# A graph layer with 400,000 edges on one core: gates computed from PSUM, last sums and maps in another order, tile bases kept in PSUM

## The chip, the cores and the metric

The kernel runs on one core of one Trainium2 chip. The metric is device time in microseconds (us) of one launch; the number given for a kernel is the median of its runs. The engines are PE (TensorE, matrix multiplies), DVE (VectorE), ACT (ScalarE), POOL (GpSimd) and SP (SyncE, which here only starts DMAs). PEld is the weight load of PE.

## The reference

12,500 nodes have 64 scalars and 32 vectors of three components (160 numbers). 400,000 edges, sorted by destination, each have a source, a destination, four numbers (e0 and the vector e1) and 64 numbers that go through a small network to 224 weights w1 to w5. Cut to what matters:

```python
h_s = s @ lin1_ws * a * _inv(64);  h_v = einsum('nci,cd->ndi', v, lin1_wv) * a * _inv(32)
w = silu(edge_scalars @ fc_w1 * _inv(64)) @ fc_w2 * _inv(64)     # split into w1..w5
es, ev = h_s[edge_src], h_v[edge_src]                            # the gather
mid_s = [w1*es*e0,  w4*(ev.e1)*_inv(3)]
mid_v = [(w2*es) x e1,  w3*ev*e0,  w5*cross(ev, e1)*_inv(2)]
agg = segment_sum(mid, edge_dst) / 4                             # the scatter
pre = sc(node) * a + lin2(agg) * a
out = [silu(pre_s[:64]),  sigmoid(pre_s[64:96]) * pre_v]         # 64 + 96 numbers
return layernorm(x + out)
```

## The kernel before

**Stages.** The first stage reads the nodes in seven chunks, multiplies them by lin1 on PE, scales the result on DVE and writes a table `h_tab` of [12500, 160] to DRAM. Between the chunks, `bases` takes the first destination of each group of three edge tiles ("block", 1042 of them), and a matmul with a row of ones spreads them over the partitions; ACT copies the result to the SBUF tile `lo` (L307, L308). When all destinations `dt` are loaded, `rel = dt - lo` (L402, L407) gives every edge its place in a window of 16 nodes.

**The loop.** Edges go in 3125 tiles of 128, in 782 steps of four tiles (the last step has one). The instruction order on PE, DVE, ACT, POOL and SP is written out by hand (`manual_schedule`). A step n does:

- `gather`: four indirect DMAs on POOL (L456), one row of `h_tab` per edge, into one of four buffers `hg`. In 11 of the 782 steps, SP fetches the rows with single DMAs instead (L485).
- `weights`: four matmuls into the PSUM tile `pw` (L498), from `hid`, which `hidden` made two steps earlier (L447 on PE, Silu on ACT, L449).
- `one_hot` (L561), `products` (L508 once, L516 three times) and `select_quad` (L570) on DVE: the 13 pieces of the messages in `pr`, and a selector `sel` with the edge's four numbers.
- `sum_up`: eight matmuls (L577) that add the tiles to `pa`, two steps behind their weights: in step n PE runs `weights(n)` and then the sums of step n - 2.
- When a pair of blocks is complete, ACT copies it (`sa`, L790); PE turns it (L586) two steps later, ACT copies that to `tt` (L589, L591).
- When sixteen blocks are turned, `output` maps the group by lin2 (22 matmuls, L601, copy `os` L604), and DVE adds each block to the window of `acc` that the block's base names (L609). The last groups are cut after the blocks at which 28, 18, 8, 2 and 0 blocks are left.

**Finishing nodes.** `finish` makes a job of four node tiles (24 jobs in the loop, the last of them with two tiles, and one behind it). `turn(k)` transposes one tile of `acc` into the PSUM tile `pp` (L636); one tile is turned per step. The step's DVE list then has, between L508 and the first L516, the scaling of `pp` by the node attribute into `z` in SBUF (L637). The following steps each take one item of the rest: `gates` (Sigmoid on ACT for all four tiles, L643), `gated` (L648, L649), `residual` (L657), `moments` (L662, L664), `root` (Sqrt, L668), `norm` (L672, L674) and the store. `finish` loads the residual rows `xt` when the job begins.

**PSUM.** Eight banks: two `pw` tiles of two banks each, two `pa`, and two `misc` banks taken in turn by `ph`, `pt`, `po`, `pp` and others. PE can write a `misc` bank only when the use before the last has been read.

**Edges of the order.** Behind the loop, the remaining sums, the turns and maps of the last groups, and the last finish job follow in program order.

## Time and profile before

| | |
|---|---|
| median of 3 runs | 3973.56 us (3970.84 to 3974.85) |
| profiled execution | 3976.66 us, span 3974.7 us |
| mean granted clock of PE | 0.968 |
| busy: PE, PEld, DVE, ACT, POOL | 92%, 40%, 61%, 24%, 74% |
| first and last gather start (L456) | 60.46 and 3937.20 us |
| last add to `acc` behind the loop; y of the last job complete | 3953.85; 3958.81 us |
| table loads on ACT | 48 for Silu, 25 for Sigmoid, 25 for Sqrt, 1 other; 1.283 us each |

How to read it: a line of the timeline gives start, duration, engine, line of the kernel, operation, output<-inputs and, in brackets, the idle time before it and what ended it ("issue": nothing that the profile shows). A line of the waits gives the total in us, the number of times and the longest wait. A line of the groups gives busy time, mean ns of one, and the idle time before them.

### The profile page before, as it was taken

What the parts mean: (1) busy time and instruction counts of PE and PEld (TensorE: products, weight loads), DVE (VectorE), ACT (ScalarE), POOL (GpSimd) and SP (SyncE); (2) the same over time, 40 slices, a digit from 0 to 9 for tenths busy, and PEclk for the clock granted to TensorE, in tenths of its full rate; (3) what the DMA queues carried; (4) which work ended last, traced back from release to release, by engine and by line L of the source; (5) the groups of instructions that cost most, each with busy time, mean ns of one, the idle gap of its engine ahead of it and who ended that gap; (6) DMA issues with size and microseconds to landing.
All of it is one profiled execution on the core that took longest, in us unless ns stands there. A gap on an engine that the chain in (4) does not pass through costs nothing. (4 is left out here: it accounts for less than half of the span.)

```text
span 3974.7 us, 58310 instructions
## 1 busy us (share of the span) xinstructions
PE 3659.0 (92%) x14291; PEld 1589.7 (40%) x14291; DVE 2416.5 (61%) x6607; ACT 940.7 (24%) x2463; POOL 2952.7 (74%) x3100
## 2 busy tenths in 40 slices
PE   6899998998999999899989999999999999999897
PEld 4344343343344344334334344343343443344343
DVE  5656665655665665656656556656665665665665
ACT  2222221221222222212212222222221221222222
POOL 4777777777777777777777777777777777777774
PEclk8999999999999999999999999999999999999998
DMA  8343444444444344443443444444444444444432
GB/s 231 96 106 86 111 100 105 98 103 104 99 99 110 95 102 105 100 108 89 107 112 91 105 99 99 107 99 97 110 99 106 99 103 104 99 99 108 99 95 67
DMA packets 243271, 412.51 MB, mean 104 GB/s; under 512 B 83147, under 2 KB 173575, under 8 KB 242023
## 3 DMA queue, kind: packets, MB, share of 16 engines
q0 software_dynamic: 150160, 262.93, 27.0%
q1 hardware_dynamic: 92246, 145.66, 15.6%
q8 instruction: 115, 1.88, 0.2%
q14 instruction: 236, 1.93, 0.2%
q10 hardware_dynamic: 514, 0.10, 0.0%
HBM read 392.43 MB, written 16.00 MB: 103 GB/s over the span
## 5 line engine op out<-in xcount | busy, mean ns | idle before, releaser
L456 POOL DMA_INDIRECT hg<-h_tab,idx x3081 | 2938.5, 954 | 945.3 <-issue 852.6
L498 PE MATMUL pw<-w,hid 128*128 128x448 f32 x3126 | 1367.3, 561 | 157.0 <-DVE sel L570 111.8
L577 PE MATMUL pa<-pr,sel 128*64 128x416 f32 x6250 | 1296.2, 536 | 0.0
L516 DVE TENSOR_TENSOR pr<-pw,hg 128x384 f32<-128x384 f32 x2313 | 1136.1, 546 | 0.0
L508 DVE TENSOR_TENSOR pr<-pw,hg 128x512 f32<-128x512 f32 x771 | 532.6, 691 | 914.4 <-DMA hg<-h_tab,idx 656.8
L498 PEld LDWEIGHTS pw<-w,hid 128*128 128x128 f32 x3126 | 554.7, 194 | 639.1 <-issue 465.6
L577 PEld LDWEIGHTS pa<-pr,sel 128*64 128x64 f32 x6250 | 386.9, 139 | 807.5 <-issue 797.8
L790 ACT COPY sa<-pa 128x416 f32<-128x416 f32 x521 | 263.7, 506 | 1360.4 <-PE pa L577 1357.9
L561 DVE TENSOR_TENSOR pw<-rel,iota 128x64 f32<-128x64 int16 x782 | 179.7, 230 | 535.8 <-PE pw L498 533.5
L447 PE MATMUL misc<-es,w 128*128 128x512 f32 (+1 forms) x784 | 447.2, 653 | 24.0 <-DMA es<-in_es_t_dram 20.8
L449 ACT ACTIVATE hid<-misc 128x512 f32<-128x512 f32 x392 | 233.6, 596 | 722.4 <-PE misc L447 717.8
L586 PEld LDWEIGHTS misc<-ident,sa 128*128 128x128 f32 x2084 | 239.6, 141 | 332.5 <-issue 252.5
L601 PE MATMUL misc<-tt,l 128*96 128x256 f32 (+5 forms) x1496 | 353.0, 384 | 15.2 <-DVE z L637 13.7
L586 PE MATMUL misc<-ident,sa 128*128 128x128 f32 x2084 | 329.1, 281 | 21.0 <-DVE z L637 14.1
L570 DVE TENSOR_TENSOR sel<-pw,eas 128x256 f32<-128x256 f32 x782 | 321.8, 412 | 0.0
L601 PEld LDWEIGHTS misc<-tt,l 128*96 128x96 f32 (+1 forms) x1496 | 231.5, 165 | 155.1 <-issue 76.5
L589 ACT COPY tt<-misc 128x192 f32<-128x192 f32 x521 | 164.8, 316 | 537.4 <-PE misc L586 524.3
L447 PEld LDWEIGHTS misc<-es,w 128*128 128x128 f32 x784 | 118.7, 191 | 286.7 <-issue 227.1
L609 DVE TENSOR_TENSOR acc<-acc,os 96x32 f32 x1042 | 195.4, 187 | 24.3 <-ACT os L604 6.0
L591 ACT COPY tt<-misc 128x64 f32<-128x64 f32 x521 | 116.5, 224 | 0.0
L604 ACT COPY os<-misc 96x512 f32<-96x512 f32 (+2 forms) x68 | 38.3, 564 | 321.6 <-PE misc L601 309.7
L636 PE MATMUL misc<-ident,acc 96*128 96x96 f32 x196 | 36.3, 272 | 55.7 <-DVE pw L561 33.3
(87 smaller groups left out, 680.6 us busy)
## 6 DMA issues: line engine op xcount, KB each, us to landing
es<-in_es_t_dram SPq DMA_DIRECT2D x258, 384.0 KB
hq<-h_tab SPq DMA_DIRECT2D x5632, 0.6 KB
hg<-h_tab,idx POOLq DMA_INDIRECT x3081
h_tab<-ht POOLq DMA_DIRECT2D x6, 1280.0 KB
xt<-in_x_dram SPq DMA_DIRECT2D x23, 320.0 KB
out_dram<-y SPq DMA_DIRECT2D x23, 320.0 KB
xv<-in_xv_t_dram SPq DMA_DIRECT2D x25, 187.5 KB
xs<-in_xs_t_dram SPq DMA_DIRECT2D x25, 125.0 KB
```

The lines of the kernel that those rows point to most:

```text
L447: nc.tensor.matmul(ph[:k, c], w1[:k, :k], es[:k, t0 * P + c0 * P:t0 * P + c1 * P], start=True, stop=True)
L449: nc.scalar.activation(hid[:k, c], ph[:k, c], AF.Silu, scale=1.0 / math.sqrt(64))
L456: nc.gpsimd.indirect_dma_start(out=hg[:, t, :], out_offset=None, in_=h_tab, in_offset=bass.IndirectOffsetOnAxis(ap=i, axis=0))
L498: nc.tensor.matmul(pw[:, t:t + m, :NWT], hid[:m * S, c * P:(c + 1) * P], w2[:m * S, :m], start=True, stop=True)
L508: nc.vector.tensor_mul(two, pw[:, :n, :2 * S].rearrange("p t (k c) -> p t k c", k=2), hg[:, :n, None, :S].to_broadcast([P, n, 2, S]))
L516: nc.vector.tensor_mul(pr[:, :n, first:first + V3].rearrange("p t (i c) -> p t i c", i=3), pw[:, :n, None, 2 * S + k * V:2 * S + (k + 1) * ...
L570: nc.vector.tensor_mul(sel[:, :n], oh[:, :, None, :].to_broadcast([P, n, 4, W]), by_slot(tiles[0][0])[:, u:u + n, :, None].to_broadcast([P ...
L577: nc.tensor.matmul(pa[half * ROWS:(half + 1) * ROWS, :NPR], sel[:, t].rearrange("p k w -> p (k w)"), pr, start=start, stop=stop)
L586: nc.tensor.transpose(pt[:, four * P:four * P + k], sa[:k, c:c + P], ident[:k, :k])
L601: nc.tensor.matmul(po[:, k, :nb], l2[r, terms[to, part, four]], a[:, :nb], start=(n == 0), stop=(n == len(of) - 1))
L609: nc.vector.tensor_add(window, window, os[:, :, b])
L790: nc.scalar.copy(sa, pas.pop(j)[:, :NPR])
```

## The change

It does five things.

- `lo` is a PSUM tile. The matmuls that spread the bases run behind the node stage, the copies on ACT are gone, and L402 and L407 read PSUM.
- `turn(k)` puts Tanh of half the scaled sums straight from `pp` into `g` (SBUF), one call per tile, and returns `gate`: three fused operations on DVE, the first two writing to free columns of the same PSUM bank. sigmoid(z) = (1 + tanh(z/2)) / 2, so (g + 1) * pp, times half the node attribute, plus `xt`, is the residual sum. `z`, `gates`, `gated` and `residual` are gone. A job has its turns and three more items.
- From step 778 on, sums run one step behind their weights.
- In step 780 (n + 2 == 782) no maps and no turns are issued; they follow in step 781, behind the last weights.
- The groups of blocks with 2 and 0 left become one.

```diff
-    lo = ends_pool.tile([P, NB], F32, name="lo")
+    base_f = ends_pool.tile([1, NB], F32, name="base_f")
...
-            for b0 in range(0, NB, U * P):
-                b1 = min(NB, b0 + U * P)
-                ps = nps.tile([P, U, P], F32, name="hp").rearrange("p u c -> p (u c)")
-                nc.tensor.matmul(ps[:, :b1 - b0], ones, base_f[:, b0:b1], start=True, stop=True)
-                nc.scalar.copy(lo[:, b0:b1], ps[:, :b1 - b0])
...
+    lo_ps = ends.enter_context(tc.tile_pool(name="lo_ps", bufs=1, space=PSUM))
+    lo = lo_ps.tile([P, -(-NB // 512) * 512], F32, name="lo")
+    for b0 in range(0, NB, 512):
+        b1 = min(NB, b0 + 512)
+        nc.tensor.matmul(lo[:, b0:b1], ones, base_f[:, b0:b1], start=True, stop=True)
     load_chunk(0, nc.gpsimd)
     nc.gpsimd.dma_start(dt, dst)
+    half_at = consts.tile([P, NT], F32, name="half_at")
+    nc.vector.tensor_scalar_mul(half_at, at, 0.5)
...
-            pp = psum.tile([P, 2, V3], F32, name="pp", tag="misc")
+            pp = psum.tile([P, 512], F32, name="pp", tag="misc")
             for m in range(2):
-                nc.tensor.transpose(pp[:, m], acc[:, m, c:c + P], ident[:V3, :V3])
-            return lambda: nc.vector.tensor_scalar(
-                z[:, k], pp.rearrange("p m c -> p (m c)"), at[:, t0 + k:t0 + k + 1], None,
-                op0=OP.mult)
...
+                nc.tensor.transpose(pp[:, m * V3:(m + 1) * V3], acc[:, m, c:c + P], ident[:V3, :V3])
+            half = half_at[:, t0 + k:t0 + k + 1]
+            nc.scalar.activation(g[:, k], pp[:, :V3], AF.Tanh, scale=half)
+            pg = pp[:, 2 * V3:2 * V3 + D]
+
+            def gate():
+                nc.vector.scalar_tensor_tensor(pg[:, :S], g[:, k, :S], 1.0, pp[:, :S],
+                                               op0=OP.add, op1=OP.mult)
+                nc.vector.scalar_tensor_tensor(
+                    pg[:, S:].rearrange("p (c i) -> p i c", i=3),
+                    g[:, k, None, S:].to_broadcast([P, 3, V]), 1.0,
+                    pp[:, V3:2 * V3].rearrange("p (i c) -> p i c", i=3),
+                    op0=OP.add, op1=OP.mult)
+                nc.vector.scalar_tensor_tensor(y[:, k], pg, half, xt[:, k],
+                                               op0=OP.mult, op1=OP.add)
...
-            if len(turns) == NO or NB - 2 * j - 2 in (28, 18, 8, 2, 0):
+            if len(turns) == NO or NB - 2 * j - 2 in (28, 18, 8, 0):
...
-                if len(waits) > 2:
+                while len(waits) > (2 if n + 4 < len(steps) else 1):
                     sum_up(n, *waits.pop(0))
                 hide(n + 2)
-                for blocks, in due(maps_due, n):
-                    output(n, blocks)
-                for j, sa in due(turns_due, n):
-                    turn_blocks(n, j, sa)
+                if n + 2 != len(steps):
+                    for blocks, in due(maps_due, n):
+                        output(n, blocks)
+                    for j, sa in due(turns_due, n):
+                        turn_blocks(n, j, sa)
```

More of the change, by code (lines that the diff above doesn't have):

```diff
@@ L301, in bases @@
             nc.vector.tensor_copy(rows[:, even:], dt[0:1, even * BT:(NB - 1) * BT + 1:BT])
-            base_f = ends_pool.tile([1, NB], F32, name="base_f")
             nc.vector.tensor_copy(base_f, rows)
-            for b0 in range(0, NB, U * P):
-                b1 = min(NB, b0 + U * P)
-                ps = nps.tile([P, U, P], F32, name="hp").rearrange("p u c -> p (u c)")
-                nc.tensor.matmul(ps[:, :b1 - b0], ones, base_f[:, b0:b1], start=True, stop=True)
-                nc.scalar.copy(lo[:, b0:b1], ps[:, :b1 - b0])
             nc.vector.tensor_sub(share, rows, share)
@@ L615, in finish @@
         whole = nt if p == P else nt - 1
-        spans = [(0, nt)] if t0 + nt == tiles_of_nodes else [(k, k + 1) for k in range(nt)]
         xt = fin.tile([P, most, D], F32, name="xt", bufs=2)
@@ L629, in turn @@
                 held.extend(fin.tile([P, most, *shape], F32, name=name) for name, shape in (
-                    ("z", [2 * V3]), ("sg", [V3]), ("y", [D]), ("st", [6]), ("mv", [2]),
-                    ("rs", [])))
-            z = held[0]
+                    ("g", [V3]), ("y", [D]), ("st", [6]), ("mv", [2]), ("rs", [])))
+            g, y = held[:2]
             c = (t0 + k) * P
-            pp = psum.tile([P, 2, V3], F32, name="pp", tag="misc")
+            pp = psum.tile([P, 512], F32, name="pp", tag="misc")
@@ L635, in turn @@
             for m in range(2):
-                nc.tensor.transpose(pp[:, m], acc[:, m, c:c + P], ident[:V3, :V3])
-            return lambda: nc.vector.tensor_scalar(
-                z[:, k], pp.rearrange("p m c -> p (m c)"), at[:, t0 + k:t0 + k + 1], None,
-                op0=OP.mult)
-        def gates():
-            z, sg = held[:2]
-            nc.scalar.activation(sg[:, :nt], z[:, :nt, :V3], AF.Sigmoid)
-        def gated():
-            z, sg, y = held[:3]
-            for k, m in spans:
-                nc.vector.tensor_mul(y[:, k:m, :S], z[:, k:m, :S], sg[:, k:m, :S])
-                nc.vector.tensor_mul(
-                    y[:, k:m, S:].rearrange("p t (c i) -> p t i c", i=3),
-                    z[:, k:m, V3:].rearrange("p t (i c) -> p t i c", i=3),
-                    sg[:, k:m, None, S:].to_broadcast([P, m - k, 3, V]))
@@ L654, in residual @@
-        def residual():
-            y = held[2]
-            for k, m in spans:
-                nc.vector.tensor_add(y[:, k:m], y[:, k:m], xt[:, k:m])
+                nc.tensor.transpose(pp[:, m * V3:(m + 1) * V3], acc[:, m, c:c + P], ident[:V3, :V3])
[12 more added lines that the diff above has]
+                                               op0=OP.mult, op1=OP.add)
@@ L659, in moments @@
+            return gate
         def moments():
-            _, _, y, st, mv, _ = held
+            _, y, st, mv, _ = held
             for k in range(nt):
@@ L666, in root @@
         def root():
-            mv, rs = held[4:]
+            mv, rs = held[3:]
             nc.scalar.activation(rs[:, :nt], mv[:, :nt, 1], AF.Sqrt, bias=eps)
         def norm():
-            _, _, y, _, mv, rs = held
+            _, y, _, mv, rs = held
             nc.vector.reciprocal(rs[:, :nt], rs[:, :nt])
@@ L679, in finish @@
         return [lambda k=k: turn(k) for k in range(nt)] + [
-            gates, gated, residual, moments, root, norm]
+            moments, root, norm]
     tiles_of_nodes = -(-N // P)
```

## The prediction

> **What bounds the kernel now.** I read the page first, then the waits of each engine, then single stretches of the timeline.

> ```profile
> PE 3659.0 (92%) x14291; PEld 1589.7 (40%) x14291; DVE 2416.5 (61%) x6607; ACT 940.7 (24%) x2463; POOL 2952.7 (74%) x3100
> ...
> L456 POOL DMA_INDIRECT hg<-h_tab,idx x3081 | 2938.5, 954 | 945.3 <-issue 852.6
> ```

> PE is busy 92%, so it looks like the bound. But look at POOL: 3081 gathers of 954 ns, with 945 us idle "before" them that nobody caused. The waits of POOL between 1000 and 2000 us say what that idle time is:

> ```profile
> POOL hg L456 <- issue: 220.2, 722, 0.3
> POOL hg L456 <- DMA hg<-h_tab,idx: 4.9, 16, 0.3
> POOL hg L456 <- DVE acc L609: 4.6, 15, 0.3
> ```

> The third number is the longest wait: 0.3 us everywhere. Every gather starts 0.30 us after the one before it ended; POOL never waits for a free buffer. The first starts at 60.46, the last at 3937.20: 3080 steps of 1.2587 us, where the usual step is 0.947 (median) + 0.305 = 1.252. So the stream of gathers carries 3877 of the 3974.7 us. The time is three terms: when the first gather starts, how long each takes, and the tail behind the last.

> PE comes second. Its waits from 400 to 3890 us (first lines):

> ```profile
> PE pw L498 <- DVE sel L570: 100.1, 65, 5.1
> PE pw L498 <- DVE acc L609: 32.3, 19, 5.2
> ...
> PE misc L601 <- DVE z L637: 13.7, 5, 4.4
> PE misc L586 <- DVE z L637: 13.7, 5, 4.6
> ```

> The list of 400 to 3890 sums to 230 us over 90 finished node tiles, 2.55 us of PE slack per tile. PE keeps up, with little to spare.

> What makes a gather long? The timeline of POOL and DVE at one finishing job:

> ```profile
> 1956.30 0.95 POOL L456 DMA_INDIRECT hg<-h_tab,idx  x1 [0.30 <-issue]
> ...
> 1957.38 0.21 DVE L648 TENSOR_TENSOR y<-z,sg 128x64 f32<-128x64 f32 x1
> 1957.52 0.29 DVE L649 TENSOR_TENSOR y<-z,sg 128x96 f32<-128x96 f32 x1
> 1957.56 2.08 POOL L456 DMA_INDIRECT hg<-h_tab,idx  x1 [0.30 <-issue]
> ...
> 1958.87 0.69 DVE L508 TENSOR_TENSOR pr<-pw,hg 128x512 f32<-128x512 f32 x1
> 1959.48 1.48 DVE L516 TENSOR_TENSOR pr<-pw,hg 128x384 f32<-128x384 f32 x3
> 1959.94 0.95 POOL L456 DMA_INDIRECT hg<-h_tab,idx  x1 [0.30 <-issue]
> ```

> The gather that falls into the eight back-to-back products of `gated` takes 2.08 instead of 0.95. Those products read two SBUF operands. The longer run L508, three L516, L570, with one operand in PSUM, leaves gathers at 0.95. At the start it is the same:

> ```profile
> 67.98 6.38 DVE L402 TENSOR_TENSOR rel<-dt,lo 128x260 int16<-128x260 int32 x12 [14.47 <-DMA dt<-in_dst_dram]
> ...
> 72.81 2.35 POOL L456 DMA_INDIRECT hg<-h_tab,idx  x1 [0.30 <-issue]
> ```

> I went through all 3081 gathers: 74 take over 0.965 us. Above the median, 39 of them lie on L648, L649 or L657 and lose 16.2 us; the four beside L402 (1.29, 1.25, 1.26, 2.35) lose 2.4; the rest, scattered, 1.6.

> **Gates from PSUM.** Removed per tile: L637 (407 ns), L648 (214), L649 (281), L657 (315) = 1.217 us of DVE, the last three with two SBUF operands. Added: one Tanh on 128x96 and three fused operations. No row shows the fused operation: at the price of the plain products it is 214 + 281 + 315 = 0.81 us; at twice the cost per element (1.04 ns by L516, 546 ns for 384) it is 0.81 + 320 x 1.04 ns = 1.14. I take 0.81, since its sizes are those of the rows. DVE saves 0.08 to 0.41 us per tile, worth nothing itself: it is 61% busy. What counts is the operands: the new three read pp, pp and pg in PSUM, with one SBUF tensor each (g, g, xt). By L508, L516 and L570 such operations don't slow a gather, so the 16.2 us go. Bounds: 0 (the slowing is not about operands) to -16.2.

> [...]

> **The longer hold.** pp's bank is one of two in the `misc` rotation. Before, it came free after L637; now after Tanh and three operations: +0.40 (0.81 - 0.41) to +0.73 us per tile. Tanh itself (0.3 us; L643 takes 362 ns for twice the columns) runs while DVE does L561 and L508 (0.9 us). Behind the gate on DVE are the three L516 of that step, and PE's next transposes or maps wait for the bank. Per tile 0.73 stays under PE's 2.55 us. Locally I compared each step's gathers with the end of the products that free their buffer: the margin is 10.6 us in the median, but 0.73 at 2432.5, 1.66 at 82.97, 2.25 at 2437.5 and 2.65 at 1178. Four turns in a row cost up to 2.9 us, so those late places lose 0 to 3 us: I take +1. The gate also needs xt five steps earlier than L657 did. Two of the 25 loads go out only at the first turn (1145.3, 3526.3); in both the next L508 stood idle 6.50 and 5.72 us for its gather, which covers it.

> Table loads: 25 sigmoids in batches become 98 separate Tanh. If Tanh needs its own table beside Silu, that is up to two loads of 1.283 us per tile, 196 loads in place of 50, ACT +187 us, on an engine 24% busy. The Silu reload at 379.64 ended 0.6 us before its operand came, so such loads hide; I take 0.

> [...]

> **Bases in PSUM.** L402 loses one SBUF operand. The four gathers get 2.4 us back, but the 17th gather (82.97) needs the buffer that step 0's products free at 79.92 + 1.47 = 81.39. So 1.5 us count. Its cost: the three banks of `lo` lie under the later pw banks, so the first L498 waits for rel (74.7) instead of running at 68.53. It took 3.35 us there, giving 78.1, and DVE is in the l2 scaling until 79.06: covered. If hid's bank is blocked too, add L447 (2.05) and Silu (0.6 + 0.2): 80.9, step 0 ends 83.2, and the 17th gather slips 0.3. Bounds -2.4 to +0.5; I take -1.5. The broadcast of the bases leaves the node stage, where PE stood from 26 to 33 us; but DMA is at 1.01 to 1.04 of its engines from 10 to 60 us, so the first gather moves by -1.4 (the wait of the last chunk, 51.22) to +1. I take 0. The three copies L308 (1.35 us of ACT) and half_at (one DVE operation in a 14 us wait) cost nothing.

> **Tail.** Counted from 3941.09, when DVE ends step 780. Before, PE had used its wait for that to run ten blocks' maps (3937.23 to 3940.79); then 18 sums, maps (2.44), transposes, maps again (2.31), last add at 3953.85. After, the sums of 779 and the last weights come earlier, but the ten blocks' maps stand behind the sums of 780: 1.62 + 3.56 + transposes 1.2 + last sums 0.4 gives 3947.9. Then copy 0.51, transposes 0.6, copies 0.54, one set of maps 2.44, copy 0.35, eight adds 1.65, gaps 0.3: 3954.3, 0.45 later. The last job took 4.96 us from there to y (3958.81). Now: transposes 0.6, Tanh 0.3, four gates of 0.81 with banks in turn, about 4.35. So -0.6 + 0.45, about -0.2. The queue is long and I modelled it by hand: -2 to +2.

> **Sum.** -16.2 - 1.5 + 1.0 - 0.2 = -16.9 us. The profiled run took 3976.66 (span 3974.7 and 2.0 around it), 3.1 above the median 3973.56; so 3959.8 there, and 3956.7 as a median.

> **Rivals.**
> A, the gathers stay slow: the cause is bursts of short DVE operations, or any use of the second SBUF operand. For it: L561 and L609 also have two SBUF operands, 180 + 195 us busy; if the 20.2 us were spread by busy time, the 82 us that go (94 x 0.81 + 6.4) would return only 3.6. Against it: the long gathers sit on L648 to L657 and L402. Time 3970 to 3974, say 3971.
> B, slower: the bank hold. If Tanh and the Silu behind it each bring an unhidden load (2.57 us) on top of 0.40 to 0.73, PE loses 3.0 to 3.3 per tile. It decides from 2.55 us on: then PE sets the pace, and 94 x (0.45 to 0.75) = 42 to 70 us are added. A cold restart makes it worse: after a 3.06 us wait for z the 22 maps at 2417.86 took 9.81 us, not 5.25. Time about 4030. Against it: loads ran ahead of their operands.
> C, the mechanism holds but the start takes no part and the thin places lose 3: 3961. This lies inside the main case.

> **How the numbers follow.** Main case (with C) 0.80, from 3951.5 (-16.2 - 2.4 - 1.4 - 2) to 3965 (-16.2 + 0.5 + 3 + 1 + 2, rounded up for gathers that stay long). A 0.11, B 0.09. The range reaches a little into A: 3951.5 to 3968. Within 0.2% means 3965.6 to 3981.5, about what a measurement of this kernel can tell from no change: that is A. Faster 0.80, same 0.11, slower 0.09.

> **What would show it.** Right: L456 near 2919 us busy for 3081 gathers, none over 1.3 us in the loop; about 3860 us from first to last gather; POOL's longest wait still 0.3; L561 of step 0 still near 79; the last add some 16 us behind the last gather, as now (16.7 from 3937.20). Wrong: gathers of 1.5 to 2 us beside the new gates (A); POOL waiting microseconds for products, PE waits for the gate growing past 200 us, table loads near 200 (B).

## The result, and the profile after

The changed kernel takes 3962.65 us (median of 11 runs, 3961.70 to 3964.88), against 3973.45 us (11 runs, 3970.57 to 3977.09) for the kernel before in the same comparison. The ratio is 0.9974, 95% interval 0.9965 to 0.9984: 10.8 us less, where 16.9 were forecast. The time lies in the range (3951.5 to 3968). Its profiled execution took 3963.18 us, span 3961.2.

The groups of the page, PE's total and POOL's gathers:

```profile
PE 3650.1 (92%) x14269; PEld 1583.0 (40%) x14269; DVE 2411.7 (61%) x6519; ACT 898.7 (23%) x2484; POOL 2932.3 (74%) x3100
...
L457 POOL DMA_INDIRECT hg<-h_tab,idx x3081 | 2918.0, 947 | 947.7 <-issue 844.0
```

The mean of a gather fell from 954 to 947 ns, that is from 2938.5 to 2918.0 us in all. Of 3081 gathers, 54 take more than 0.965 us, and together they lose 3.4 us; before, 74 lost 20.1. None takes more than 1.10. The timeline at one of the new gates shows why:

```profile
1937.16 0.34 ACT L637 ACTIVATE g<-misc,half_at 128x96 f32<-128x96 f32 x1 [1.09 <-PE misc L635]
1937.22 0.95 POOL L457 DMA_INDIRECT hg<-h_tab,idx  x1 [0.30 <-issue]
1937.87 0.22 DVE L641 SCALAR_TENSOR_TENSOR misc<-g,misc 128x64 f32<-128x64 f32 x1
1938.12 0.26 DVE L643 SCALAR_TENSOR_TENSOR misc<-g,misc 128x96 f32<-128x96 f32 x1
1938.42 0.38 DVE L648 SCALAR_TENSOR_TENSOR y<-misc,half_at,xt 128x160 f32<-128x160 f32 x1
1938.48 0.95 POOL L457 DMA_INDIRECT hg<-h_tab,idx  x1 [0.30 <-issue]
```

Both gathers lie on the gate's operations and keep their 0.95 us.

The waits of POOL from 64 to 3950 us (total, times, longest):

```profile
POOL hg L457 <- issue: 837.3, 2747, 0.3
POOL hg L457 <- DMA hg<-h_tab,idx: 28.0, 92, 0.3
POOL hg L457 <- DVE pr L517: 20.4, 59, 2.8
```

The last line is new: one gather waited 2.8 us for a buffer. It is the 17th; the timeline of the start, with its cause:

```profile
74.05 0.43 DVE L408 TENSOR_TENSOR rel<-dt,lo 128x1 int16<-128x1 int32 x5
74.58 2.04 PE L448 MATMUL misc<-es,w 128*128 128x512 f32 x2 [18.88 <-DVE rel L408]
77.31 3.35 PE L499 MATMUL pw<-w,hid 128*128 128x448 f32 x4 [0.69 <-ACT hid L450]
80.70 0.23 DVE L562 TENSOR_TENSOR pw<-rel,iota 128x64 f32<-128x64 int16 x1 [1.86 <-PE pw L499]
81.57 1.48 DVE L517 TENSOR_TENSOR pr<-pw,hg 128x384 f32<-128x384 f32 x3
83.32 0.94 POOL L457 DMA_INDIRECT hg<-h_tab,idx  x1 [2.75 <-DVE pr L517]
```

Not only the first weights but already the first `hid` (L448) waits until `rel` is done, so step 0's products end at 83.05, and the 17th gather starts behind them.

The waits of PE, 400 to 3880 us:

```profile
PE pw L499 <- DVE sel L571: 56.0, 38, 4.0
PE misc L635 <- DVE pw L562: 54.6, 23, 6.2
...
PE misc L587 <- DVE y L648: 12.9, 8, 4.6
PE misc L602 <- DVE y L648: 11.1, 8, 4.6
```

With 7.6 us of L635, the waits for the gate come to 31.6 us; those for `z` were 37.9. Table loads are 25 for Silu, 25 for Sqrt and 1 other: 98 Tanh added none.

Last, the tail. In the timeline:

```profile
3919.58 0.64 PE L499 MATMUL pw<-w,hid 64*128 64x224 f32 x2
3923.19 3.04 PE L578 MATMUL pa<-pr,sel 128*64 128x416 f32 x8 [2.97 <-DVE pw L562]
3926.16 3.59 PE L602 MATMUL misc<-tt,l 128*96 128x160 f32 x22
...
3937.89 1.74 DVE L610 TENSOR_TENSOR acc<-acc,os 96x32 f32 x8 [4.56 <-ACT os L605]
```

and the windows of that wait and of the sums behind it (busy PE, PEld, DVE, ACT, POOL, then granted clock, DMA share, GB/s):

```profile
3920.22:3923.19 2.97, 0.00 (x1) 0.04 (x1) 2.53 (x7) 0.00 (x0) 0.00 (x0) 0.94 0.50 136
3923.19:3926.20 3.01, 3.01 (x9) 0.86 (x9) 1.08 (x6) 0.00 (x0) 0.00 (x0) 0.50 0.12 23
```

PE waited 2.97 us with nothing to do, the clock was halved behind the wait, and the eight sums of step 780 took 3.04 us instead of 1.62. From the last gather (3919.11) to the last add's end (3939.63) it is 20.5 us; before, 16.65.

### The profile page after: what moved, and what is told of

It is laid out like the page before. It is cut to its first block, busy times and chain, and to the rows that moved or that the text cites. A ratio compares the mean times of both kernels' runs of the same rounds, so it can differ in the third digit from the quotient of the medians.

```text
span 3961.2 us, 58261 instructions
## 1 busy us (share of the span) xinstructions
PE 3650.1 (92%) x14269; PEld 1583.0 (40%) x14269; DVE 2411.7 (61%) x6519; ACT 898.7 (23%) x2484; POOL 2932.3 (74%) x3100
## 5 line engine op out<-in xcount | busy, mean ns | idle before, releaser
L457 POOL DMA_INDIRECT hg<-h_tab,idx x3081 | 2918.0, 947 | 947.7 <-issue 844.0
L499 PE MATMUL pw<-w,hid 128*128 128x448 f32 x3126 | 1360.3, 559 | 116.7 <-DVE sel L571 66.6
L517 DVE TENSOR_TENSOR pr<-pw,hg 128x384 f32<-128x384 f32 x2313 | 1137.4, 547 | 0.0
L499 PEld LDWEIGHTS pw<-w,hid 128*128 128x128 f32 x3126 | 553.8, 194 | 593.9 <-issue 469.3
L562 DVE TENSOR_TENSOR pw<-rel,iota 128x64 f32<-128x64 int16 x782 | 179.4, 229 | 538.7 <-PE pw L499 536.9
L448 PE MATMUL misc<-es,w 128*128 128x512 f32 (+1 forms) x784 | 451.4, 658 | 24.1 <-DVE rel L408 18.9
L448 PEld LDWEIGHTS misc<-es,w 128*128 128x128 f32 x784 | 119.7, 192 | 287.8 <-issue 231.6
L610 DVE TENSOR_TENSOR acc<-acc,os 96x32 f32 x1042 | 194.3, 187 | 29.4 <-ACT os L605 11.1
L635 PE MATMUL misc<-ident,acc 96*128 96x96 f32 x196 | 36.4, 271 | 87.1 <-DVE pw L562 62.0
```

The costliest lines, as they stand in the source:

```text
L448: nc.tensor.matmul(ph[:k, c], w1[:k, :k], es[:k, t0 * P + c0 * P:t0 * P + c1 * P], start=True, stop=True)
L457: nc.gpsimd.indirect_dma_start(out=hg[:, t, :], out_offset=None, in_=h_tab, in_offset=bass.IndirectOffsetOnAxis(ap=i, axis=0))
L499: nc.tensor.matmul(pw[:, t:t + m, :NWT], hid[:m * S, c * P:(c + 1) * P], w2[:m * S, :m], start=True, stop=True)
L517: nc.vector.tensor_mul(pr[:, :n, first:first + V3].rearrange("p t (i c) -> p t i c", i=3), pw[:, :n, None, 2 * S + k * V:2 * S + (k + 1) * ...
L610: nc.vector.tensor_add(window, window, os[:, :, b])
```

## Theories for the experiments

T1: gathers are long where DVE runs back to back through operations with two SBUF operands; the gates from PSUM end that. T2: the rest of the change gives some of it back, by PE's wait in the tail, in which the clock falls. Rivals: gathers are slowed by any use of two SBUF operands, or by any burst (A); the longer hold of the banks costs (B). Some of the runs below were made on chips on which the kernel before takes 5254 to 5338 us, so each is compared only with runs of the kernel before on the same chip. Line numbers of the experiments' kernels differ by a few from those of the changed kernel.

## Experiment 1: the gates alone

The kernel before with the new `turn`, `gate` and `half_at` only:

```diff
+            nc.scalar.activation(g[:, k], pp[:, :V3], AF.Tanh, scale=half)
...
+                nc.vector.scalar_tensor_tensor(y[:, k], pg, half, xt[:, k],
+                                               op0=OP.mult, op1=OP.add)
```

> The gates alone, for a chip on which the kernel before takes about 3,972 us. If the gathers' loss is what the gates free: no gather over 1.1 us beside the gate operations, about 3 us lost in all instead of 20, last gather near 3,919 to 3,921, 16.6 us from the last gather to the last add as before, time 3,956 to 3,960. If the gathers are slow whatever DVE reads: 3,971. On a chip of the other sort: from no difference to 0.4% slower, as before.

Measured: 3958.10 us (6 runs, 3956.44 to 3958.93) against 3970.66 (10 runs); ratio 0.9968, interval 0.9956 to 0.998. The page's group of gathers:

```profile
L458 POOL DMA_INDIRECT hg<-h_tab,idx x3081 | 2916.5, 947 | 944.7 <-issue 839.5
```

50 gathers over 0.965 us lose 3.3 us, none is above 1.10 beside a gate. Three at 1.25 to 1.26 are left at the start, where the operation on `rel` still reads two SBUF tensors; the whole change has none there. The last gather starts at 3915.88, 3 us earlier than forecast, with no wait of POOL above 0.3 us. So the gates alone bring 22.0 us of gather time, 16.8 of it from gathers over 0.965 us, and the whole gain. That the old gates made gathers long and the new ones don't is shown by an edit that touches nothing else; A's time, 3971, is refuted. Which property of the old gates did it is not shown by this run. The edit moves an operand to PSUM, but it also breaks up the run of eight products, and the new operations no longer overlap: L641 takes 0.22 us and the next begins 0.25 later, where L648 took 0.21 and the next began 0.14 later. Experiments 3 and 5 tell these apart in part.

The tail was a miss: 19.7 us from the last gather to the last add, not 16.6. Not the order, but the clock: three groups that ran at full clock before now run at half. The last of them, before and with the gates alone, each with the wait ahead of it:

```profile
3929.99 0.43 PE L447 MATMUL misc<-es,w 64*64 64x128 f32 x2 [1.73 <-ACT hid L449]
3930.34 1.77 PE L498 MATMUL pw<-w,hid 128*128 128x448 f32 x4
```

```profile
3910.13 0.59 PE L449 MATMUL misc<-es,w 64*64 64x128 f32 x2 [1.73 <-ACT hid L451]
3910.65 3.25 PE L500 MATMUL pw<-w,hid 128*128 128x448 f32 x4
```

The weights lose 1.48 us; sums at 3896.32 took 2.80 instead of 1.62 and the two hidden matmuls at 3899.05 took 1.59 instead of 1.13, behind a wait of 2.19 us at a turn that was 0.27 before. These three are 3.1 us, and the tail grew by 3.1, though not by them alone: one wait of 0.44 us went, and the gathers ended 0.5 us earlier against PE's work.

```profile
3925.61:3929.02 3.41, 2.65 (x12) 0.78 (x10) 1.18 (x6) 1.27 (x2) 2.50 (x4) 1.00 0.27 65
3929.02:3932.43 3.41, 2.44 (x8) 1.06 (x10) 3.32 (x12) 1.17 (x3) 2.50 (x4) 1.00 0.23 55
```

```profile
3906.85:3910.26 3.41, 1.68 (x9) 0.57 (x6) 2.70 (x7) 2.17 (x3) 2.52 (x3) 1.00 0.26 69
3910.26:3913.67 3.41, 3.41 (x6) 1.24 (x5) 0.00 (x0) 0.27 (x1) 2.50 (x4) 0.50 0.19 54
```

Before, the wait (3928.26 to 3929.99) is split between two stretches, and PE is busy for 2.65 and 2.44 us of them. With the gates alone it lies whole in one (3908.40 to 3910.13), PE is busy for 1.68 of 3.41 us, and the next stretch has half clock. From 150 us to 60 us before the end, the traces of before, after and the gates alone have 42, 39 and 42 falls of the clock: each follows a stretch with PE busy (matmuls or weight loads) for at most 0.50 of it, and the least busy stretch without a fall had 0.42. So the share of one stretch that the waits fill goes with the fall, not the length of the one wait.

The same kernel on four other chips:

> The gates from PSUM alone, in the kernel before; bases and tail as before. Theory (two SBUF operands on DVE slow a gather on POOL): no gather over 1.2 us beside the gates, so first to last gather falls from 3876.7 to about 3860 us; the four long gathers beside the place computation at 68 to 75 us stay (2.4 us); the tail from the last gather to the last add stays 16.6 us. Time 3956 to 3960 us. Rival (bursts of short DVE operations slow a gather, whatever their operands): long gathers of 1.4 to 2 us remain beside the gates and the time is 3969 or more. Rival (the longer hold of the PSUM bank costs): POOL waits for products inside the loop and the time is above 3965.

| kernel before, us | gates alone, us | ratio, 95% interval |
|---|---|---|
| 5260.16 | 5274.86 | 1.0032 (1.0003 to 1.0061) |
| 5254.17 | 5277.77 | 1.0039 (1.0014 to 1.0064) |
| 5337.94 | 5346.25 | 1.0016 (0.9996 to 1.0037) |
| 5254.89 | 5269.04 | 1.0035 (1.0015 to 1.0055) |

> The gates from PSUM alone, in the kernel before; bases and tail as before. Theory (two SBUF operands on DVE slow a gather on POOL): no gather over 1.2 us beside the gates; the four long gathers at 68 to 75 us stay (2.4 us); first to last gather 3859 to 3862 us; last gather to last add 16.6 us as before. Time 3956 to 3960 us. Rival (bursts of short DVE operations slow a gather, whatever their operands): long gathers remain beside the gates, 3969 or more. Rival (the longer hold of the PSUM bank costs): POOL waits for products inside the loop, above 3965.

> The gates alone in the kernel before (tanh of the sums in PSUM and the fused gate operations; the bases stay in SBUF, the old places of the last sums and maps). If the gathers' loss is what the gates free, and the chip is one on which the kernel before takes about 3,972 us: no gather over 1.1 us beside the gate operations, gathers lose about 3 us in all instead of 20 (four of those left at the start, beside the scaling that waits for rel), last gather near 3,919 to 3,921, tail 16.6 us from the last gather to the last add as before, time 3,956 to 3,960. If the gathers are slow whatever DVE reads: 3,971. If the longer hold of the banks is passed on: 4,000 or more. On a chip where the kernel before takes about 5,255 us: 0.3 to 0.4% slower, as in the two tries so far.

> The gates alone once more, for a chip on which the kernel before takes about 3,972 us. If the gathers' loss is what the gates free: no gather over 1.1 us beside the gate operations, about 3 us lost in all instead of 20, last gather near 3,919 to 3,921, the tail 16.6 us from the last gather to the last add as before, time 3,956 to 3,960. If the gathers are slow whatever DVE reads: 3,971. On a chip of the other sort (5,255 to 5,340 us): from no difference to 0.4% slower, as in the three tries so far.

The gathers' loss falls here too (1.8, 1.7, 1.6 and 2.0 us in all, most of it at the start), but it buys nothing. The waits of POOL on the first of these chips, 1000 to 2000 us, and the first of DVE's:

```profile
POOL hg L458 <- DVE pr L518: 253.6, 55, 17.6
POOL hg L458 <- issue: 165.3, 526, 1.7
```

```profile
DVE pw L563 <- remote: 239.5, 28, 13.2
DVE pw L563 <- PE pw L500: 119.4, 52, 7.5
```

POOL waits for products, products wait for PE and for releases that the trace can't place ("remote"), and PE's mean clock is 0.87 instead of 0.97. PE itself is busy only 76% of the span there, against 92%; what holds it up isn't shown. Where gathers don't set the pace, their gain is worth nothing, and the gates cost 0.2 to 0.4% (in the third row the interval reaches 1). That B's hold of the banks is that cost is not shown.

## Experiment 2: the maps back in step 780

The changed kernel without its guard:

```diff
-                if n + 2 != len(steps):
-                    for blocks, in due(maps_due, n):
-                        output(n, blocks)
-                    for j, sa in due(turns_due, n):
-                        turn_blocks(n, j, sa)
+                for blocks, in due(maps_due, n):
+                    output(n, blocks)
+                for j, sa in due(turns_due, n):
+                    turn_blocks(n, j, sa)
```

> The changed kernel with one line undone: the maps of ten blocks and the turn that fall due in step 780 are issued there again, in front of the last weights; sums one step behind and one group less stay. Theory (PE waits with nothing in front of it, and comes out of the wait at half clock): the maps fill the wait, the eight sums of step 780 take 1.6 us instead of 3.04, and the last add comes 9 to 12 us behind the last gather instead of 20.5; time 3953 to 3957 where the changed kernel has 3962.65. Rival (the new order as such was right, and the loss lies elsewhere): last add later than 20 us behind the last gather, time 3962 or more.

Measured: 3956.94 us (5 runs, 3955.25 to 3957.34) against 3970.62 (9 runs); ratio 0.9964, interval 0.995 to 0.9977. The timeline:

```profile
3919.97 3.56 PE L602 MATMUL misc<-tt,l 128*96 128x160 f32 x22
3924.52 1.62 PE L578 MATMUL pa<-pr,sel 128*64 128x416 f32 x8
3929.35 2.98 PE L602 MATMUL misc<-tt,l 128*96 128x128 f32 x22 [0.52 <-ACT tt L592]
3932.81 1.74 DVE L610 TENSOR_TENSOR acc<-acc,os 96x32 f32 x8 [4.87 <-ACT os L605]
```

The maps now fill PE's wait, the sums run at full clock (1.62 us), and the last add ends 14.9 us behind the last gather (3919.61) instead of 20.5; 9 to 12 were forecast. T2 is shown in the traces: this guard alone cost the changed kernel 5.6 us of tail. The medians differ by 5.7 us too, though in two comparisons; each against its own kernel before, it is 13.7 against 10.8 us, and the two intervals overlap. At the start the 17th gather waited 3.96 us here, and one more wait of 1.19 came at 2892.6. This is the lowest median of all; gates alone (0.9968) can't be told from it. Gates alone with this tail was not tried.

## Experiment 3: the other two parts, each alone, and two together

The kernel before with the order of the end alone, then with the bases in PSUM alone:

```diff
-                if len(waits) > 2:
+                while len(waits) > (2 if n + 4 < len(steps) else 1):
...
+                if n + 2 != len(steps):
...
-            if len(turns) == NO or NB - 2 * j - 2 in (28, 18, 8, 2, 0):
+            if len(turns) == NO or NB - 2 * j - 2 in (28, 18, 8, 0):
```

```diff
-    lo = ends_pool.tile([P, NB], F32, name="lo")
+    lo = lo_ps.tile([P, -(-NB // 512) * 512], F32, name="lo")
```

The third kernel has the gates and the bases, without the order of the end.

> The new order of the last sums, turns and maps alone, in the kernel before. Theory (PE waits about 3 us for the products of step 780 with nothing in front of it, runs the next sums at half clock, and has the ten blocks' maps still before it): last gather to last add about 20.5 us instead of 16.6, so the kernel is 3 to 5 us slower, 3977 to 3978.5. Rival (the prediction's count): last add 0.4 us later, the last job 0.6 us shorter, time 3973.3.

> The bases in PSUM alone, in the kernel before. Theory (the first hidden matmul waits until rel is complete, step 0 ends late, and the 17th gather waits about 2.5 us, which eats the 2.4 us that the four gathers beside the place computation get back): 17th gather near 83.3 us, time equal to before within 0.5 us, 3973 to 3974. Rival (the prediction's -1.5): 17th gather near 81.5 us, time 3972.

> The change without its tail: gates and bases new, last sums, turns and maps in the order of before. Theory: last gather near 3919, last add 16.6 us behind it, about 4 us faster than the changed kernel: 3957 to 3959. Rival (the lost part of the gain lies in the loop or at the start, not in the tail): about 3962.5, as the changed kernel.

These ran on the chip of the table's first row, where gathers don't set the pace; of the forecast times nothing can be judged. Measured: order alone 5258.15 (ratio 1.0000, 0.997 to 1.003), bases alone 5259.45 (0.9986, 0.9955 to 1.0016), gates and bases 5281.32 (1.0037, 1.0009 to 1.0065). The tail that was forecast for the order alone can't be judged either: PE's wait ahead of the sums of step 780 was 0.75 us there, not 3, and the sums ran at full clock (1.62 us). What counts is which gathers over 0.965 us are left in each trace:

| | lost, us | of it before 85 us | at finishing jobs |
|---|---|---|---|
| order alone | 10.4 | 1.3 | bursts of 1.2 to 1.7 |
| bases alone | 10.0 | 0.2 | bursts of 1.2 to 2.0 |
| gates alone | 1.8 | 1.0 | none |
| gates and bases | 0.6 | 0.1 | none |

Each loss goes with its own edit: bases with the one at the start, gates with the one at the jobs. At the start only the place of `lo` changes; the operations on `rel`, their shapes and their pace stay. On the chip of the result, in the trace after:

```profile
67.91 6.24 DVE L403 TENSOR_TENSOR rel<-dt,lo 128x260 int16<-128x260 int32 x12 [12.13 <-DMA dt<-in_dst_dram]
72.12 0.94 POOL L457 DMA_INDIRECT hg<-h_tab,idx  x1 [0.30 <-issue]
```

Before, the same twelve operations took 6.38 us with both operands in SBUF, and the four gathers beside them lost 2.4 us; with `lo` in PSUM they lose nothing. So here the second SBUF operand is shown to be what made gathers long. No timed run tells what the bases and the order alone are worth where gathers set the pace.

## Experiment 4: the first hidden matmul freed from `rel`

```diff
-        misc_ps = Banks(banks, "misc", 512, 2)
+        misc_ps = Banks(misc_banks, "misc", 512, 2)
```

> The changed kernel with the maps of step 780 issued there again, and the two misc banks in a pool of their own, which doesn't lie over the bases' pool. Theory (the first hidden matmul waits for rel only because the banks' pool as a whole lies over the bases): that matmul runs near 65 us instead of 74.58, the first weights matmul near 74.6, step 0's products end near 81.3, the 17th gather starts near 81.4 instead of 83.32; 1.5 to 2 us faster than the same kernel without the split (3956.94): 3955. Rival (the wait is on the data of the first tile only, wherever the banks lie): 17th gather still near 83.3, 3957.

The kernel of experiment 2, with the `misc` banks in a pool of their own. Before that, the banks of the loop were one pool, laid over the banks of `lo`; L448 waits for `rel` because of the pool, not because of its own bank. With the `misc` banks apart:

```profile
65.90 2.04 PE L448 MATMUL misc<-es,w 128*128 128x512 f32 x2 [10.68 <-DMA es<-in_es_t_dram]
76.20 3.33 PE L499 MATMUL pw<-w,hid 128*128 128x448 f32 x4 [8.26 <-issue]
```

L448 runs at 65.90 instead of 74.58, and L499 starts 0.15 us behind `rel` (76.05) instead of 2.8. That the pool was the cause is shown. The time, 5270.91 against 5254.17 (1.0031, 1.0007 to 1.0055), was measured on the second chip of the table; there DVE ran the scaling L265 in pieces, with waits between them, until 85.4, so step 0 came no earlier. What this is worth on the first kind of chip is open.

## Experiment 5: spare products beside the gathers

Eight unused products of 128x96 ahead of each gate of the changed kernel, with two SBUF operands or with one in PSUM:

```diff
             def gate():
+                for _ in range(8):
+                    nc.vector.tensor_mul(spare, g[:, k], xt[:, k, :V3])    # or pp[:, :V3]
```

> The changed kernel with eight spare products of 96 columns in front of each gate, both operands in SBUF (g and xt), result unused. Theory (two SBUF operands): gathers beside them take 1.3 to 2.3 us; at the rate of before (0.43 us lost per run of 1.24 us of such products) 94 runs of 1.4 us lose 40 us or more; POOL's busy time for gathers above 2945 us, time near 4000. Rival (bursts, not operands): the same loss as in the kernel with one operand in PSUM.

> The same eight spare products with one operand in PSUM (g and the transposed sums). Theory (two SBUF operands): no long gathers, POOL's busy time stays near 2918 us; the bank is held about 1.4 to 2 us longer per tile, under the 2.55 us of slack per tile, so the time stays within 4 us of the changed kernel, 3962 to 3967. Rival (bursts): as slow as with both operands in SBUF, 4000. Rival (bank hold): POOL starts to wait for products, 10 us or more.

Measured, on the second chip of the table: 5313.49 us with SBUF (ratio 1.0104, 1.0057 to 1.0151), 5309.82 with PSUM (1.0116, 1.0066 to 1.0166). The groups:

```profile
L643 DVE TENSOR_TENSOR spare<-g,xt 128x96 f32<-128x96 f32 x784 | 202.2, 258 | 61.9 <-DMA xt<-in_x_dram 21.1 <-ACT g L638 13.4 <-issue 3.2
```

```profile
L643 DVE TENSOR_TENSOR spare<-g,misc 128x96 f32<-128x96 f32 x784 | 198.4, 253 | 47.1 <-ACT g L638 19.6 <-issue 3.6
```

In the traces, 188 gathers lie on SBUF products and lose 2.6 us in all, 14 ns each; 190 lie on PSUM products and lose nothing (-0.06 us). So the operand does make a difference, as T1 says, but a loss near 40 us was forecast: two SBUF operands in a burst are not enough. The bursts differ in one more thing. The first line is from the run with SBUF, the others from the kernel before:

```profile
1936.91 2.29 DVE L643 TENSOR_TENSOR spare<-g,xt 128x96 f32<-128x96 f32 x8
```

```profile
1663.31 1.02 DVE L657 TENSOR_TENSOR y<-y,xt 128x160 f32<-128x160 f32 x4
1663.54 1.75 POOL L456 DMA_INDIRECT hg<-h_tab,idx  x1 [0.30 <-issue]
```

The spare products write one tile in turn. One takes 0.258 us and eight take 2.29, so there is a gap of about 0.03 us behind each. L657 takes 0.315 us and four take 1.02, so each begins about 0.08 us before the one ahead of it ends; so do L648 and L649, and the twelve of L402 (0.61 us each, 6.38 in all). L657 has no strided operand and L402 no fast pace, so long gathers need neither. What fits every row is two SBUF operands together with operations that overlap: L403 and L517 overlap too, with one operand in PSUM, and gathers beside them stay at 0.95. No run changed the overlap alone. If this reading is right, the new gates, which don't overlap, would have lost little with SBUF operands too.

The spare products add about 2.3 us per tile and cost 0.7 to 0.9% beyond the kernels with gates and bases but without them (1.0031 in experiment 4, 1.0037 in experiment 3). They hold the bank, as rival B has it, but they also delay the products of L517 behind them, for which POOL waits on these chips; the two are not told apart.

Beside a lone operation with two SBUF operands a gather loses little: with L562 (0.23 us), 739 gathers of the changed kernel lose 5 ns each on average.

## Why the prediction was right, and where it was not

All terms are differences of the two profiled executions, after less before, in us:

| step of the sum | forecast | measured | from |
|---|---|---|---|
| gathers themselves: gates -16.2, four at the start -2.4 | -18.6 | -20.5 | L457 busy 2918.0, L456 2938.5 |
| start: first gather, wait of the 17th | +0.9 | +2.7 | 60.75 for 60.46; 2.75 for 0.30 |
| thin places of the longer hold | +1.0 | 0 | no other wait above 0.36 |
| other gaps between gathers | 0 | -0.3 | the rest to 3919.11 for 3937.20 |
| last gather to last add | +0.45 | +3.9 | 20.5 for 16.65 |
| last job up to y | -0.6 | -0.2 | 4.75 for 4.96 |
| y to the end of the span | 0 | +0.9 | 16.8 for 15.9 |
| sum | -16.9 | -13.5 | spans 3961.2 and 3974.7 |

**Right: the bound, and where the gathers lose.** The time follows the stream of gathers, and the gathers that lost were those on the old gates. The reason given, two SBUF operands, is shown at the start (experiment 3); at the gates it is one of two things that the edit changed (experiment 5). The term came out 2 us larger than forecast, and that is not the mechanism: gathers over 0.965 us give 16.7 us back, and the other 3.8 are about 1.2 ns for each of the rest. Runs differ by as much in this (medians of 946 to 949 ns). The gate takes 221 + 262 + 384 ns = 0.867 us, between the bounds of 0.81 and 1.14 and near the value taken (the upper bound's 1.04 ns per element is L516's step from 247 ns for 96 elements to 546 for 384). The plain products of the same shapes, with both operands in SBUF, took 214, 281 and 315: L641 is 7 ns longer, L643 19 shorter and L648 69 longer. What part the reading of PSUM has in this isn't shown. Tanh takes 341 ns (0.3 forecast) and no table load, so the up to two loads of 1.283 us per tile that the prediction allowed for, and that B counted as unhidden, didn't come.

**Mis-sized: the start.** -1.5 was taken for the whole of it (-2.4 + 0.9). The alternative that the text gave, hid's bank blocked too, is what happened: step 0 ended at 83.05 (83.2 was worked out there), and the 17th gather started 83.32, 0.35 later than before. Where the pool's banks lie was left unread and the milder case taken. With the 2.4 us back and 2.7 lost, the start took no part; POOL's longest wait of 0.3 us, one of the signs of being right, didn't hold.

**Mis-sized: the tail.** The hand model ran every matmul at full clock. The sums behind the 2.97 us wait ran at 0.50, +1.4; the last sums came another 1.3 us late behind two sets of transposes with a wait of 0.97 for the copies between; and the last maps, of eight blocks, took 2.98 instead of 2.44. The bound for the tail with the last job was +2; it cost +3.7, and the sign "some 16 us" became 20.5. The prediction had a row for it, 22 maps that took 9.81 instead of 5.25 us after a wait of 3.06, and used it for rival B only. PE was not idle for the whole of a stretch ahead of the falls here: of 3.41 us it was busy for 0.80 (the tail of the change), 1.22 and 1.68 us (the gates alone).

**The step from the profile to the median.** 3.1 us were taken off as if the kernel kept that distance. Before, the profiled run lay 3.2 above the median of its comparison; after, 0.5. So 13.5 us in the profiles are 10.8 in the medians. That the losses of the long gathers differ from run to run is a guess that fits.

Rival A's outcome fell with experiment 1. Of its two causes, any use of two SBUF operands fell already with L562 and L610 in the changed kernel's trace (739 and 536 gathers beside them lose 4 to 5 ns each), and any burst with L403 and L517, which run back to back with one operand in PSUM (the gathers beside them take 945 and 947 ns on average); bursts of operations with two SBUF operands remain. Rival B fell on the chip of the result, where neither loads nor the hold made POOL wait in the loop; on the others the change of the gates was slower, as B said, but its cause there is not shown. C's sum, 3961, was nearest to the time, but for other reasons: the start took no part, yet the thin places cost nothing, and the tail did. The sum came nearer to the forecast than its terms, and that is luck: the gathers' 1.9 us beyond the forecast and the thin places' 1.0 made up for part of what the start (1.8) and the tail (3.5) took.

## What to carry to other kernels

Find the stream whose steps follow one another without waits and look at its longest single instructions, not at the engine with the highest busy share: what lay beside them on another engine cost some 17 to 19 us of 3974 here, with DVE's busy time almost unchanged. Look there for operations with two SBUF operands that overlap one another: gathers beside such operations took up to 2.35 us here instead of 0.95. Keep PE fed in the tail of a kernel: here a wait of 2.97 us cost itself and a clock of 0.50 behind it, at which eight sums took 3.04 us instead of 1.62; with maps in that wait the tail was 14.9 us instead of 20.5. So work that is ready belongs into the wait, even if it could be done later. And read the sign on the chip that counts: where gathers didn't set the pace, the same edit made the kernel slower.

## What the runs showed that was not expected

- The same program takes 3971 us on some chips and 5254 to 5338 on others, with PE busy 76% instead of 92%, its mean granted clock at 0.86 to 0.87 instead of 0.97, and DVE waiting for releases that the trace doesn't place.
- One wait of 1.73 us of PE is followed by clock 1.00 in one run and 0.50 in another: in the first it lies across two stretches of 3.41 us, with PE busy for 2.65 and 2.44 us of them, in the other whole in one, with PE busy for 1.68.
- Silu and Tanh alternate on ACT with no table load between them: 98 Tanh, 25 loads for Silu, as many as there were Sqrt groups.
- Of two bursts of products with two SBUF operands, the one whose operations overlap made a gather take up to 2.08 us, the other 14 ns more on average.
